# A two-layer graph network: the leftover nodes as row tiles of their own, in all stages

## The chip, the cores and the metric

One core of a Trainium2 chip runs the whole program. The metric is the time of one execution in microseconds (us). "Before" is the kernel as it was, "changed" the kernel under study. All runs quoted have one core, so there is no second die to compare.

## The reference, cut to what matters

```python
# x: 2708 nodes x 1024 features, float32; adj: 2708 x 2708 int32
# layer 0
h = relu(layernorm(x))
f = h @ Wf + bf;  g = h @ Wg + bg
att = softmax(where(adj > 0, relu(f @ g.T), NEG), axis=1)
x = x + att @ (h @ W + bW)
# layer 1
h = relu(layernorm(x));  hw = h @ W1
e = leaky_relu(hw @ a1 + (hw @ a2).T)
x = x + relu(softmax(where(adj > 0, e, NEG), axis=1) @ hw)
```

2708 is 21 x 128 + 20. The 21st full tile and the last 20 nodes are what the change is about.

## The kernel before

Output nodes are taken in five *panels*. For each panel the kernel makes the query side (stage Q), the scores against all nodes (S), the attention-weighted sum of the rows of h (G, "aggregation") and the product with W (P, "projection"). Layer 1 has only G and P. Q, S, G and P are Strassen products of halves: seven products m (M1 to M7) in place of eight. The matmuls of these products are float32, and the trace shows each as two instructions.

Panels were 586, 586, 512, 512, 512 wide. 586 is four tiles of 128 and one of 74:

```python
    wide = (N - 3 * W) // 2                 # 586
    width = [wide, wide, W, W, W]
    ...
    short = [t for t in range(NT) if tiles[t][1] < P]     # the two tiles of 74 rows
    n0, n1 = (tiles[t][1] for t in short)                 # 74, 74
    NM = P - n0                                           # 54
    NY = n1 - NM                                          # 20
    LEFT, MONO, TINY = NQ, NT, NT + 1
```

As *input* rows (of the scores and the aggregation) the 148 leftover nodes were regrouped: MONO is 74 + 54 = 128 rows, TINY the last 20. As *output* rows of the projection they stayed two tiles of 74, a Strassen pair of their own:

```python
        if p == panel_of[short[1]]:
            n = tiles[short[1]][1]
            todo.append((*short, n, [carry[:, e, :, :n] for e in range(2)], col(full, n)))
```

So layer 1's f2 of those nodes (the dot product of a row with a vector) was made in one arrangement and used in the other, and small DMAs carried it over:

```python
    def left_f2():
        a, b = (f[1][:, t:t + 1] for t in short)
        store(f[1][:n0, MONO:MONO + 1], a[:n0])
        store(f[1][n0:, MONO:MONO + 1], b[:NM])
        for g in range(P // B32):
            store(f[1][B32 * g:B32 * g + NY, TINY:TINY + 1], b[NM:n1])
        nc.vector.tensor_scalar(f2s[:, MONO:], f[1][:, MONO:], ALPHA, None, op0=OP.mult)
```

Row work like this is kept in a list (`put`) and handed out in small portions (`behind`) between the matmuls of the next stage. In the scores VectorE keeps the order in which the program names its instructions. A *unit* of the scores is one pair of node tiles: eleven a panel, the last of them MONO and TINY. A *spread* is a transpose on TensorE that lays a column of numbers out as a row on all partitions.

The adjacency matrix becomes additive masks, transposed on TensorE; the part of a panel beyond four full tiles is a *tail*:

```python
            if tail:
                ps = bank("mk_ps", (P, 2, W), BF)
                for k in range(2):
                    nc.tensor.transpose(ps[:, k, :tail], m[1][:tail, 0, k], identb[:tail, :tail])
```

## Time and profile before

| | before |
|---|---|
| median (range) of four runs | 3178.63 us (3177.99 to 3184.48) |
| span of the profiled run | 3178.7 us |
| TensorE idle in it | 3178.7 - 3089.0 = 89.7 us |

"Busy" is the union of an engine's instructions in time. A line number such as L1018 is that of the kernel the profile belongs to, so one place has two numbers: the scores are L1018 before and L1052 after; L45 is a helper through which every VectorE instruction goes, so its tile name tells what it is. In the waits, the line reads: who waited, for whom, total us, times, longest us.

### The profile page before, as it was taken

The page shows a single profiled execution, that of the slowest core. Times are in us where ns is not written, and L with a number is a line of the kernel's source. Part 1 is how long each engine was busy: PE and PEld are TensorE (multiplying, and loading weights), DVE is VectorE, ACT ScalarE, POOL GpSimd, SP SyncE. Part 2 cuts the span into 40 slices and gives each one's busy share as a digit, 9 for nine tenths or more (in the row PEclk, how much of TensorE's full clock was granted, in tenths as well). Part 3 has the DMA queues.
Part 4 walks back from the last instruction along what each step waited for, and adds up shares of the span by engine and source line. Part 5 has one row for each costly group of instructions (what it writes and reads, how often), then busy time and mean ns, then how long its engine had stood idle before and what let it go on. Part 6 is the DMA issues. An engine that isn't in the chain of part 4 may idle for free.

```text
span 3178.7 us, 35524 instructions
## 1 busy us (share of the span) xinstructions
PE 3089.0 (97%) x12982; PEld 2283.8 (72%) x12982; DVE 1782.1 (56%) x3561; ACT 504.2 (16%) x855; POOL 406.7 (13%) x547
## 2 busy tenths in 40 slices
PE   8998999999999989999999999997999999999998
PEld 5576677667876578886888885864767748778684
DVE  7867576375722665517672357657574472644612
ACT  4412120010200101101020002203131130211200
POOL 3724102110002220011000101021010000000000
PEclk9999999999999989999999999998999999999999
DMA  6857839676446566567755567596555455665655
GB/s 248 325 204 281 276 133 340 202 243 211 149 125 185 184 226 204 154 199 238 245 173 154 165 203 228 195 301 221 201 169 178 143 171 170 192 200 171 214 157 196
DMA packets 272487, 649.76 MB, mean 204 GB/s; under 512 B 38016, under 2 KB 104584, under 8 KB 272312
## 3 DMA queue, kind: packets, MB, share of 16 engines
q1 hardware_dynamic: 231320, 523.52, 51.7%
q0 software_dynamic: 40992, 123.96, 11.2%
q8 instruction: 103, 1.69, 0.2%
q14 instruction: 72, 0.59, 0.1%
HBM read 534.53 MB, written 112.83 MB: 204 GB/s over the span
## 4 chain that ended last, share of the span: by engine, by line
PE 86%; issue 6%; DVE 3%; DMA 2%; POOL 1%; ACT 0%; SPq 0%; POOLq 0%; DVEq 0%; ACTq 0%
PE gy L537 11%; PE gz L537 11%; PE gx L537 11%; PE sz L1018 7%; PE pz L916 6%; PE sy L1018 5%; PE gv L537 5%; PE sx L1018 4%; PE px L916 4%; PE py L916 4%; PE M_ps L469 3%; PE qz L537 3%; PE qx L537 2%; PE qy L537 2%; PE mk_ps L693 1%
## 5 line engine op out<-in xcount | busy, mean ns | idle before, releaser
L1018 PE MATMUL sz<-B,As 128*128 128x256 f32 (+1 forms) x1200 | 296.5, 396 | 4.6 <-DVE st L45 3.4
L1018 PEld LDWEIGHTS sz<-B,As 128*128 128x128 f32 x1200 | 229.2, 192 | 53.3 <-DVE st L45 4.8
L1018 PE MATMUL sx<-B,As 128*128 128x256 f32 (+1 forms) x800 | 203.1, 397 | 16.6 <-DVE sm L45 11.5
L849 POOL TENSOR_TENSOR gT<-gT,rr 128x2048 f32<-128x2048 f32 (+3 forms) x20 | 69.8, 3491 | 1144.1 <-DVE rr L45 1056.6
L1018 PE MATMUL sy<-B,As 128*128 128x256 f32 (+1 forms) x800 | 201.7, 395 | 4.8 <-DVE st L45 4.8
L537 PE MATMUL gz<-P,hc 128*128 128x256 f32 (+1 forms) x800 | 186.0, 393 | 2.3 <-ACT gT L838 2.3
L537 PE MATMUL gz<-Sa,hc 128*128 128x256 f32 (+1 forms) x800 | 186.0, 393 | 2.3 <-ACT gT L838 2.3
L537 PE MATMUL gx<-P,hc 128*128 128x256 f32 (+1 forms) x800 | 184.4, 392 | 0.3 <-ACT P L1330 0.3
L537 PE MATMUL gy<-T,hc 128*128 128x256 f32 (+1 forms) x800 | 184.2, 391 | 0.0
L1018 PEld LDWEIGHTS sx<-B,As 128*128 128x128 f32 x800 | 149.3, 191 | 45.7 <-DVE sm L45 11.9
L1018 PEld LDWEIGHTS sy<-B,As 128*128 128x128 f32 x800 | 152.2, 191 | 37.3 <-DVE st L45 5.9
L537 PEld LDWEIGHTS gz<-Sa,hc 128*128 128x128 f32 x800 | 151.2, 190 | 36.0 <-ACT gT L838 4.5
L537 PEld LDWEIGHTS gz<-P,hc 128*128 128x128 f32 x800 | 150.9, 190 | 35.7 <-ACT gT L838 4.5
L537 PEld LDWEIGHTS gx<-P,hc 128*128 128x128 f32 x800 | 152.1, 190 | 32.7 <-issue 2.0
L537 PEld LDWEIGHTS gy<-T,hc 128*128 128x128 f32 x800 | 151.7, 190 | 30.9
L916 PE MATMUL py<-w,ps 128*128 128x512 f32 (+1 forms) x352 | 155.7, 593 | 0.0
L916 PE MATMUL pz<-w,ps 128*128 128x512 f32 (+1 forms) x352 | 155.1, 592 | 0.0
L694 ACT COPY mask<-mk_ps 128x1024 bf16<-128x1024 bf16 x55 | 55.7, 1013 | 615.0 <-PE mk_ps L693 274.3
L916 PE MATMUL px<-w,gT 128*128 128x512 f32 x320 | 144.3, 605 | 6.4 <-issue 5.8
L916 PEld LDWEIGHTS pz<-w,ps 128*128 128x128 f32 (+1 forms) x352 | 65.4, 186 | 85.6 <-issue 82.0
L916 PEld LDWEIGHTS py<-w,ps 128*128 128x128 f32 (+1 forms) x352 | 65.2, 186 | 85.2 <-issue 80.3
L916 PEld LDWEIGHTS px<-w,gT 128*128 128x128 f32 x320 | 60.8, 193 | 83.6 <-issue 80.3
(319 smaller groups left out, 4997.6 us busy)
## 6 DMA issues: line engine op xcount, KB each, us to landing
hc<-hg_d SPq DMA_DIRECT2D x350, 512.0 KB
As<-hs_d SPq DMA_DIRECT2D x150, 512.0 KB
w<-wt_d SPq DMA_DIRECT2D x96, 512.0 KB
w<-in_L_gnn_W_dram SPq DMA_DIRECT2D x72, 512.0 KB
md<-md_d SPq DMA_DIRECT2D x56, 512.0 KB
adj_i<-in_adj_dram SPq DMA_DIRECT2D x50, 512.0 KB
hg_d<-g POOLq DMA_DIRECT2D x40, 512.0 KB, 5.2
hs_d<-hsT POOLq DMA_DIRECT2D x40, 512.0 KB, 6.1
```

The source lines that it names most:

```text
L469: nc.tensor.matmul(ps, wfT[a][c // NH][:, c % NH, :], wgT[b][c], start=(c == 0), stop=(c == NC - 1))
L537: nc.tensor.matmul(ps[d], left(m, k, d), right(m, k), start=(start and k == 0), stop=(k == K - 1 and m not in more), skip_group_check=True)
L693: nc.tensor.transpose(ps[:, k, i * P:(i + 1) * P], m[0][:, i, k], identb)
L694: nc.scalar.copy(mk[:, :, :k4 * P], ps[:, :, :k4 * P])
L849: nc.gpsimd.tensor_tensor(of(e, s), of(e, s), by(s, k), OP.mult)
L916: nc.tensor.matmul(ps, left[i][m][:, k, :], w_[k], start=(start and k == 0), stop=(k == NH - 1), skip_group_check=True)
L1018: nc.tensor.matmul(ps[:n, :h], lefts[q][:, i % 2, c, :n], B[m][c // 2][:, c % 2, :h], start=(start and c == 0), stop=(c == NH - 1), skip_g ...
```

## The change

Its intent: make the leftover nodes the same tiles everywhere. MONO is 64 nodes of panel 1 and 64 of panel 2, TINY 20 nodes of panel 3, as input rows *and* as output rows. Then the third Strassen pair of 74 rows becomes one plain tile of 128 (four products) and one of 20, and f2 needs no copies.

```diff
-    wide = (N - 3 * W) // 2
-    width = [wide, wide, W, W, W]
+    NM = P // 2
+    NY = N - NP * W - P
+    width = [W + NM, W + NM, W + NY, W, W]          # 576, 576, 532, 512, 512
 ...
+        def for_other(m, w_):
+            e, start = int(m in (M2, M3)), m in (M1, M5)
 ...
+            for k in range(NH):
+                if other == MONO:
+                    nc.tensor.matmul(ps, carry[:, e, k], w_[k], ...)
+                    continue
+                for g in range(P // B32):
+                    nc.tensor.matmul(ps[B32 * g:B32 * (g + 1)], G[e][:, k, W:W + B32],
+                                     w_[k][:, g * P:(g + 1) * P], ...)
 ...
-            put(0.0, lambda: (left_h(1, *(done_rows[s] for s in mine)), left_f2()))
+            put(0.0, lambda: left_h(1, *(done_rows[s] for s in mine)))
 ...
+        def rows_of_tiny():
+            xs[TINY] = row_halves("x_res")
+            for e in range(2):
+                nc.gpsimd.memset(xs[TINY][e], 0.0)
+                for ps, _ in places[TINY]:
+                    nc.gpsimd.dma_start(xs[TINY][e][ps], x1_d[TINY][:, e * W:(e + 1) * W])
+            rows_done(TINY, xs[TINY])
```

The inner loop over g is the "four column groups": the 20 rows are weights of 32 columns, and four such sets stand side by side in the array, each with another quarter of 128 columns of W. The result lies as four quarters on the partitions 0, 32, 64, 96, so the 20 rows go through DRAM once to become whole rows again. (The diff is cut; the rest adapts loads, stores and columns.)

## The prediction

> **What bounds the kernel now.** I began with the busy times of the page, because they say whether there is anything but TensorE to look at.
>
> ```profile
> PE 3089.0 (97%) x12982; PEld 2283.8 (72%) x12982; DVE 1782.1 (56%) x3561; ACT 504.2 (16%) x855; POOL 406.7 (13%) x547
> ```
>
> TensorE is busy for 3089.0 of 3178.7 us, so at most 90 us is idle, and the rest falls only if TensorE gets fewer columns to stream. Then I asked what a column costs. The groups by form give the busy time of each shape:
>
> ```profile
> L537 PE MATMUL gz<-P,hc 128*128 128x256 f32 x480 | 105.7, 380 | 1.4 <-ACT gT L838 1.4
> L537 PE MATMUL gz<-P,hc 128*128 128x293 f32 x320 | 80.3, 411 | 0.9 <-ACT gT L838 0.9
> L916 PE MATMUL pz<-w,gT 128*74 128x512 f32 x16 | 7.2, 592 | 0.0
> ```
>
> The 380 and 592 ns of one instruction include the pipeline, so I divide busy time by count: 105.7/480 = 220 ns for 256 columns, 80.3/320 = 251 ns for 293. Both are 0.86 ns a column, with no fixed part: five panels that add up to 2708 columns cost the same however they are cut. The third row says that a tile of 74 rows costs what one of 128 does (450 ns, with the tail of the last included). The chain in order of time gives the pace without tails:
>
> ```profile
> 1038.76 10.30 PE py L916 x24
> ...
> 1236.40 1.86 PE sz L1096 x32
> 1238.27 1.92 PE sx L1088 x8
> 1240.19 3.45 PE sy L1088 x16
> ```
>
> 24 instructions of 512 columns take 10.30 us, so 429 ns each; a product of one tile (8 instructions, two for each f32 matmul of four K blocks) is 3.43 us. The second row is the scores of the 20 nodes, done in four column groups: 32 instructions of 256 columns in 1.86 us, 58 ns each, a quarter of the 216 ns of the last row (3.45/16). The eight after it take 1.92 and not 1.73 us, so leaving the groups costs about 0.2 us.
>
> Last I looked for the 90 idle microseconds, in the waits of TensorE and then of VectorE (columns: total us, times, longest us):
>
> ```profile
> PE sx L1018 <- DVE sm L45: 11.5, 1, 11.5
> PE mk_ps L693 <- DVE nm L45: 8.0, 6, 2.7
> ...
> DVE f2s L45 <- DMA f<-f: 13.8, 1, 13.8
> ```
>
> The longest wait of all is one event, and the timeline of VectorE and GpSimd in the scores of the third panel shows its cause:
>
> ```profile
> 1156.30 0.17 DVE L45 TENSOR_SCALAR f2s<-f 128x2 f32<-128x2 f32 x1 [13.81 <-DMA f<-f]
> ...
> 1158.78 3.78 PE L1018 MATMUL sx<-B,As 128*128 128x256 f32 x8 [11.46 <-DVE sm L45]
> 1163.97 1.04 PE L693 MATMUL mk_ps<-identb,nm 128*128 128x128 bf16 x8 [1.41 <-DVE nm L45]
> ...
> 1131.43 4.07 POOL L140 DMA_DIRECT2D hgl_d<-x_res  x8 [1.58 <-ACT x_res L289]
> 1138.03 4.04 POOL L140 DMA_DIRECT2D hgl_d<-x_res  x8 [2.53 <-DMA hgl_d<-x_res]
> ...
> 1148.84 3.47 POOL L140 DMA_DIRECT2D f<-f  x7 [1.00 <-DMA hgl_d<-x_res]
> ```
>
> The 128+20 nodes left over are cut out of two tiles of 74 rows. To bring their f2 onto the right partitions the kernel copies it with twelve small DMAs, queued behind 24 small ones of the rows. VectorE takes its instructions in order; it reaches the scaling of f2 at 1142.5 and stands until 1156.3, and TensorE runs out of free accumulators: 11.46 + 1.41 = 12.9 us lost.
>
> **What the Trainium skill says.** "TensorEngine Tiling (Array Packing)", Instruction Overhead, gives about 60 cycles of overhead to each matmul, and its Key Properties say that a change of tiling mode drains the engine. The trace agrees with the second (the 0.2 us above); at 256 columns it shows no overhead, but the change goes to 128, where four groups leave 27 ns for an instruction. "TensorE: Matmul & The Clock Gate", Back-to-back issue gap, puts an issue floor of about 25 ns under small matmuls, so 27 is just possible there. "DMA: Bandwidth & Descriptors", Anatomy of one DMA, gives a DMA from GpSimd a fixed cost of about 2 us, mostly the receipt of the write. Here it is more: eight issues from 1131.43, then the next waits until 1138.03 for one of them.
>
> **The change, part by part.**
>
> 1. *Third Strassen group out of the projection.* Before, the two 74-row tiles are a pair with 7 products of 3.43 us: 24.0 us a layer, 48.0 in two. It goes, all of it on TensorE's path.
> 2. *128 nodes as a plain tile.* Four products (two K halves by two output halves) of 3.43 us: 13.7 a layer, +27.5 in two.
> 3. *20 nodes in four column groups.* Four visits a layer, each 16 matmuls of 128 columns, 32 instructions. Half of 1.86 us is 0.93, plus 0.2 for the switch: 1.13 at best. At the 58 ns of the trace it would be 2.06. I choose 1.4 (37 ns each, as small weight loads and issue take their part): 5.6 a layer, +11.2 in two.
> 4. *The same columns elsewhere.* Scores, query side and aggregation go from 293, 293, 256, 256, 256 to 288, 288, 266, 256, 256 a half; the sum is 1354 in both: 0.
> 5. *Small TensorE work.* The leftover rows are transposed as full tiles: in the chain 16 instructions took 1.03 us for 74 columns and 1.75 for 128, so +0.72 for each of two tiles, +1.4. The third panel now has a tail of 20 columns: 22 mask transposes at some 30 ns (two of 74 columns took 0.07 us) and a few spreads: +1.2.
> 6. *The twelve copies of f2 and the wait go.* The rows now lie on the partitions where f2 is used; the only copy left moves 64 values of f1, in program order nothing on VectorE waits for it soon: -12.9.
> 7. *What is added off TensorE.* The 20 nodes' rows are finished as four quarters, stored by sixteen small DMAs and fetched back by eight before they can be normalized. In the built order this hides behind other row work, but VectorE meets the statistics of that tile in the second unit of the fourth panel's scores, some 30 us after the last quarter is stored (1461 and about 1492 on the old clock). Sixteen to thirty DMAs at 0.55 us of issue and some 5 us to land are 15 to 25 us. It should just fit; I allow +2 for it and for the fuller VectorE there (96 of 138 us busy before, about 10 more after).
>
> Sum: -48.0 + 27.5 + 11.2 + 1.4 + 1.2 - 12.9 + 2 = -17.6 us. From 3179.05 that is 3161.4.
>
> **The rivals.**
>
> *The wait moves to the fourth panel.* The same mechanism, GpSimd's small DMAs ahead of an in-order VectorE instruction, is set up again by part 7. For it: only eight DMAs seem to be in flight at a time, and the round trip goes through HBM. Against it: GpSimd is busy 13% and the order leaves 30 us. If the whole chain were late by 10 us, the time would be about 3171.
>
> *Column groups that do not overlap.* If the four groups of 128 columns ran one after another, an instruction would take 107 ns (429/4), part 3 would be 8 x 3.6 = 29 and not 11 us, and the time 3179: no gain in TensorE at all. Against it stands the 58 ns of the same technique in the scores.
>
> *The stall was masking something.* Without the f2 wait, VectorE's backlog in the third panel (its row work of five tiles) could hold TensorE anyway; the tile of 20 leaves that stage, which speaks against it. Then half of the 12.9 would stay: 3168.
>
> *Everything fits*, with groups at 30 ns and no new wait: about 3156.
>
> **Range and chances.** The sure terms are 1 and 2 (-20.5); the term of the wait is nearly sure to vanish where it is, less sure not to come back. The rivals put the time between 3156 and 3179, mostly under 3172. Runs before spread by 6 us. I take 3161 with a range of 3150 to 3173. Two per cent is 63.6 us: with at most 90 us of idle and 20 us of matmuls to win, faster by over 2% is hardly possible (0.01), and no rival loses more than a few us against before (slower 0.01).
>
> **What would show it.** In the changed profile TensorE's busy time should be about 3082 (6.7 less: 48.0 - 27.5 - 11.2 - 1.4 - 1.2); the second panel's projection about 62 us where it was 73; a visit of the column groups 1.1 to 1.7 us in the timeline; the wait of f2 gone from VectorE's waits, and the 11.5 from TensorE's. Wrong would be: a new wait of VectorE for a DMA at the statistics of x_res over 3 us, a visit over 2 us, or TensorE idle by over 85 us.

## The result, and the profile after

| | before | changed |
|---|---|---|
| median of four runs, us | 3178.63 (3177.99 to 3184.48) | 3166.18 (3162.18 to 3169.59) |
| ratio | | 0.9956 (95%: 0.9939 to 0.9974) |
| profiled span, us | 3178.7 | 3160.3 |

A ratio is the mean time of one kernel's fast runs over that of the other's of the same rounds, so it is not quite the ratio of the medians. Ten later runs of the changed kernel, five on each of two chips, gave 0.9952 and 0.9954. The change is worth about half a per cent, by the verdict of 2% the same.

The busy line of the changed kernel's page:

```profile
PE 3085.6 (98%) x13218; PEld 2290.2 (72%) x13218; DVE 1768.6 (56%) x3561; ACT 505.2 (16%) x872; POOL 411.8 (13%) x552
```

TensorE's busy time fell by 3.4 us and its idle time from 89.7 to 74.7. So most of the gain is idle time, and of the 6.7 us of busy time that were forecast about half is missing. (More is missing from the matmuls: the slow stretch that followed the f2 wait before was busy time too; see b_later.) The waits of TensorE in the changed kernel, the longest three:

```profile
PE mk_ps L700 <- DVE nm L45: 9.6, 7, 3.8
PE mx_ps L739 <- DVE mx L45: 7.1, 1, 7.1
PE px L948 <- issue: 5.8, 1, 5.8
```

The 11.5 us of `sx` are gone. Now the stage where they were, the scores of the third panel, as a stretch of the trace: length, then busy time of each engine with its instructions, then the granted clock (the share of TensorE's full clock that the trace shows as granted), DMA share and GB/s. Before:

```profile
1091.20:1244.50 153.30, 139.91 (x709) 119.74 (x709) 95.73 (x202) 14.07 (x17) 29.09 (x50) 0.94 0.72 234
```

and changed:

```profile
1070.30:1215.40 145.10, 144.69 (x734) 120.09 (x733) 96.97 (x209) 15.25 (x28) 14.16 (x22) 1.00 0.74 241
```

Idle time went from 13.4 to 0.4 us although the panel is 4% wider, and the granted clock from 0.94 to 1.00.

In the projection of the third panel, the chain of the changed kernel (start, us, what) shows the column groups:

```profile
1402.99 7.06 PE px L948 x16
1410.05 1.01 PE po L925 x32
1411.06 7.06 PE px L948 x16
```

A visit (one run of these 32 instructions) is 1.01 us, and the 16 instructions after it take 7.06 and not 6.87: 1.20 us in all.

The whole by stages, each from its first TensorE instruction to that of the next, in us; "changed" is a second profile of it (run a_same, below):

| stage | before | changed | difference |
|---|---|---|---|
| S, panel 1 | 187.0 (idle 16.0) | 182.4 (idle 11.3) | -4.6 |
| S, panel 2 | 160.2 (idle 2.7) | 160.4 (idle 3.8) | +0.2 |
| P of panel 2, layer 0 and 1 | 73.14, 72.20 | 63.37, 61.90 | -9.8, -10.3 |
| S, panel 3 | 153.3 (idle 13.4) | 144.4 (idle 0.4) | -8.9 |
| G of panel 3, layer 0 and 1 | 133.02, 134.29 | 138.03, 139.35 | +5.0, +5.1 |
| P of panel 3, layer 0 and 1 | 49.11, 48.17 | 53.94, 53.00 | +4.8, +4.8 |
| S, panel 4 | 138.0 (idle 1.8) | 139.7 (idle 3.3) | +1.7 |

One row does not fit: panel 2 went from 293 to 288 columns a half, 1.7%. Its scores (157.5 us without the idle) should have become 2.7 us shorter and became 0.8 us shorter with the idle out on both sides; against the kernel "before with the wait put later" (155.8 without idle) they even grew. The chain of one unit of these scores shows why. Before, 74-row tail (the first line is the pace, 8 instructions):

```profile
743.44 1.98 PE sy L1018 x8
745.41 0.45 PE mk_ps L693 x8
745.86 0.07 PE mk_ps L698 x2
745.93 2.06 PE sx L1018 x8
```

Changed, 64-row tail:

```profile
719.23 1.94 PE sy L1052 x8
721.17 0.45 PE mk_ps L700 x8
721.61 0.16 PE mk_ps L705 x2
721.77 2.14 PE sx L1052 x8
```

The two transposes are smaller (64 x 64 in place of 74 x 74) and cost more: 0.16 and not 0.07 us, and the eight matmuls after them 0.20 and not 0.08 over their pace. A unit pays 0.36 in place of 0.15. Panel 3, which had no tail, pays for its 20 x 20 transposes too:

```profile
1108.93 0.14 PE mk_ps L705 x2
1109.07 1.99 PE sx L1052 x8
...
1123.11 1.79 PE sx L1052 x8
```

The sum over 22 units of 64 rows and 11 of 20 is 22 x 0.21 + 11 x 0.29 (0.14 + 0.20, less 0.05 that the full mask transposes leave behind without a tail) = 7.8 us. I had put 0.7 us there.

### The profile page after: what moved, and what is told of

Read it like the earlier page. It is cut to its first block, busy times and chain, and to the rows that moved or that the text cites. A ratio compares the mean times of both kernels' runs of the same rounds, so it can differ in the third digit from the quotient of the medians.

```text
span 3160.3 us, 36134 instructions
## 1 busy us (share of the span) xinstructions
PE 3085.6 (98%) x13218; PEld 2290.2 (72%) x13218; DVE 1768.6 (56%) x3561; ACT 505.2 (16%) x872; POOL 411.8 (13%) x552
## 3 DMA queue, kind: packets, MB, share of 16 engines
q0 software_dynamic: 41024, 124.12, 11.3%
## 4 chain that ended last, share of the span: by engine, by line
PE 87%; issue 6%; DVE 3%; POOL 1%; DMA 1%; ACT 0%; SPq 0%; POOLq 0%; DVEq 0%; ACTq 0%
PE gy L545 12%; PE gz L545 11%; PE gx L545 11%; PE sz L1052 7%; PE pz L948 5%; PE sy L1052 5%; PE sx L1052 5%; PE gv L545 5%; PE px L948 3%; PE M_ps L465 3%; PE qz L545 3%; PE py L948 3%; PE qy L545 2%; PE qx L545 2%; PE po L921 1%
## 5 line engine op out<-in xcount | busy, mean ns | idle before, releaser
L1052 PE MATMUL sz<-B,As 128*128 128x288 f32 (+2 forms) x1200 | 296.7, 397 | 3.2 <-DVE st L45 3.2
L856 POOL TENSOR_TENSOR gT<-gT,rr 128x2304 f32<-128x2304 f32 (+5 forms) x20 | 75.4, 3769 | 1088.4 <-DVE rr L45 1003.1
L1052 PE MATMUL sx<-B,As 128*128 128x288 f32 (+2 forms) x800 | 203.1, 397 | 3.2 <-DMA As<-hs_d 3.1
L1052 PE MATMUL sy<-B,As 128*128 128x288 f32 (+2 forms) x800 | 199.1, 392 | 3.1 <-DVE st L45 3.1
L545 PE MATMUL gz<-P,hc 128*128 128x288 f32 (+2 forms) x800 | 186.0, 393 | 2.3 <-ACT gT L845 2.3
L545 PE MATMUL gz<-Sa,hc 128*128 128x288 f32 (+2 forms) x800 | 186.0, 393 | 2.3 <-ACT gT L845 2.3
L545 PE MATMUL gx<-P,hc 128*128 128x288 f32 (+2 forms) x800 | 185.6, 394 | 0.0
L545 PE MATMUL gy<-T,hc 128*128 128x288 f32 (+2 forms) x800 | 184.2, 391 | 0.0
L948 PE MATMUL py<-w,ps 128*128 128x512 f32 x320 | 143.4, 598 | 0.0
L948 PE MATMUL pz<-w,ps 128*128 128x512 f32 x320 | 141.8, 593 | 0.0
```

Source lines behind the costliest of these rows:

```text
L545: nc.tensor.matmul(ps[d], left(m, k, d), right(m, k), start=(start and k == 0), stop=(k == K - 1 and m not in more), skip_group_check=True)
L856: nc.gpsimd.tensor_tensor(of(e, s), of(e, s), by(s, k), OP.mult)
L948: nc.tensor.matmul(ps, left[i][m][:, k, :], w_[k], start=(start and k == 0), stop=(k == NH - 1), skip_group_check=True)
L1052: nc.tensor.matmul(ps[:n, :h], lefts[q][:, i % 2, c, :n], B[m][c // 2][:, c % 2, :h], start=(start and c == 0), stop=(c == NH - 1), skip_g ...
```

## The experiments

Theory: (A) the gain is the f2 wait; it is larger than its idle time, because the clock is lower after it. (B) The projection's matmuls gain as forecast, but small transposes of 64 rows and fewer give much of it back by switching TensorE's tiling mode. Rivals: the wait was masking a backlog; the quarters of TINY cost something by their DMAs; the short instructions themselves and not the switch are dear.

The first four ran on one chip, where before had a median of 3183.0 us.

**a_same**: the changed kernel again, no edit.

> The changed kernel again, as it stands, to see its spread and to have it on the same chip as the runs that change a part of it. Its four runs so far went from 3162 to 3170 us, where before had 3178 to 3184. If the spread is chance, five more give a mean of 3164 to 3168, ratio 0.995 to 0.997.

Measured: 3165.94 us (3163.32 to 3171.15, five runs), 0.9952 (0.9940 to 0.9965). As expected. The spread of 8 us is the kernel's own; the stage that differs most between profiles of the same code is the first panel's scores (idle 11 to 17 us in the profiles). What decides that was not tried.

**b_later**: the kernel before, copies kept, the waiting instruction later.

```diff
-            put(0.0, lambda: (left_h(...), left_f2()))          # f2s scaled at the end of left_f2
+            put(0.0, lambda: (left_h(...), left_f2()))          # copies only
+            put(12.0, lambda: None)
+            put(0.0, left_f2s)
             put(0.0, met)
```

> The kernel before, with the same twelve copies of f2 but the instruction that waits for them put about two and a half units of the scores later. My theory: the 12.9 us that TensorE lost behind the 13.8 us wait of VectorE come back, and nothing else moves: about 3166 us, 0.996, and no wait of f2s for a DMA in the profile. Rival: VectorE's backlog would have held TensorE there anyway, so that about half returns: 3172, 0.998.

Measured: 3165.35 us (3163.50 to 3165.75, five runs), 0.9947 (0.9934 to 0.9959). No wait of f2s for a DMA is left. The scores of the third panel, as a stretch again:

```profile
1088.64:1225.35 136.71, 136.18 (x711) 117.54 (x709) 97.74 (x209) 14.06 (x17) 30.05 (x51) 1.00 0.79 262
```

They took 136.71 us in place of 153.31: 16.6 us, of which 12.9 is idle time. So the rival (half returns) falls, and the forecast 12.9 was too small by 3.7. Moving one instruction in the old kernel buys as much as the whole change. What the matmuls of the change gain, something else in it must lose.

**a_wait**: the changed kernel with a wait put back.

```diff
+            if k == 1 and t == MONO:
+                dot(fm, done_rows[t], halves(wab[k]))
+                for i in range(0, P, 4):
+                    nc.gpsimd.dma_start(f[1][i:i + 4, c:c + 1], fm[i:i + 4])
+            else:
+                dot(f[k][:, c:c + 1], done_rows[t], halves(wab[k]))
```

> The changed kernel with the wait put back: f2 of the tile of 128 nodes goes through 32 small DMAs of 4 rows each to its place, and VectorE scales it at once after. Theory: 32 issues at 0.5 us and 5 us of landing make a wait of 18 to 25 us on VectorE in the third panel's scores, of which TensorE loses all but 1 to 3 us: 15 to 24 us slower than the changed kernel on the same chip, so 3180 to 3190. Rival: what the change gained came from the matmuls and a wait there is absorbed: within 4 us of the changed kernel.

Measured: 3184.52 us (3181.72 to 3188.52, four runs), 1.0009 to before, 18.6 us slower than a_same. VectorE's wait, and TensorE after it:

```profile
DVE f2s L45 <- DMA f<-fm: 17.4, 1, 17.4
```

```profile
1096.92 3.91 PE L1053 MATMUL sy<-B,As 128*128 128x266 f32 x8 [14.62 <-DVE st L45]
```

A wait of 17.4 us on VectorE idles TensorE for 14.6, and the stage became 17.5 us longer (144.40 to 161.91). The eight matmuls after the gap take 3.91 us where this form takes 1.96 (the lengths of one timeline row, tails included): half speed. Theory A holds in both directions.

**a_flat**: TINY as a plain tile, without column groups.

```diff
-                for g in range(P // B32):
-                    nc.tensor.matmul(ps[B32 * g:B32 * (g + 1)], G[e][:, k, W:W + B32], w_[k][:, g * P:(g + 1) * P], ...)
+                nc.tensor.matmul(ps, G[e][:, k, W:W + B32], w_[k], ...)      # ps: 32 rows x 512
```

(The diff is cut; the rest loads, finishes and stores the rows whole.)

> The changed kernel with the 20 nodes projected as a plain tile of 32 rows by 512 columns in place of four column groups; with it they are also loaded, finished and stored by whole rows, so with fewer small DMAs. Theory: a visit of the groups costs 1.20 us in the trace of the changed kernel, four plain matmuls of 512 columns cost 3.43, so 8 x 2.23 = 17.8 us slower than the changed kernel. Rival: the small DMAs of the four quarters cost something too, and their going pays part of it back: 10 us slower or less.

Measured: 3186.09 us (3184.44 to 3187.28, four runs), 1.0013, 20.2 us slower than a_same. A visit in its chain:

```profile
1413.42 3.55 PE po L924 x8
1416.97 7.07 PE px L947 x16
```

3.55 + 0.20 (7.07 over 6.87) = 3.75 against 1.20 is 2.55 us a visit; eight are 20.4. My 17.8 left out that the plain tile of 32 columns pays at its edges as well. The rival falls: fewer DMAs paid nothing back, so the quarters cost no visible time. And the column groups are worth their trouble: without them the change is no gain.

The next four ran together on another chip, before at 3180.59 us.

**a_mask96**: the tails of the masks with 96 rows.

```diff
+        R = 96 if tail else 0
-            last = adj[r0 + k4 * P:r0 + w]
+            last = adj[r0 + k4 * P:r0 + k4 * P + R]
...
-                    nc.tensor.transpose(ps[:, k, :tail], m[1][:tail, 0, k], identb[:tail, :tail])
+                    nc.tensor.transpose(ps[:, k, :R], m[1][:R, 0, k], identb[:R, :R])
```

(The diff is cut; the loads and the negation take R rows too.)

> The changed kernel with the tails of the masks (64, 64 and 20 rows) read, negated and transposed with 96 rows, of which the first 64 or 20 are used. In the traces the two transposes of a 74-row tail and what follows cost TensorE 0.15 us a unit, those of 64 rows 0.36, those of 20 rows 0.29 where there was nothing. My theory: a tile of 64 rows or fewer puts TensorE into another tiling mode and the switch costs about 0.1 us each way; with 96 rows there is none, a unit costs about 0.17: 22 x 0.19 + 11 x 0.12 = 5.5 us faster than the changed kernel (3160.5 if that is at 3166). Rival: the extra is not the switch but the short instructions and their semaphores, or it hides behind VectorE: within 1 us of the changed kernel, or slower by the wider transposes.

Measured: 3160.14 us (3157.56 to 3162.76, five runs), 0.9933 (0.9920 to 0.9945). Against the changed kernel's 0.9952 that is 0.0019 of 3181, 6.0 us. The same unit in its chain:

```profile
722.06 1.94 PE sy L1053 x8
724.00 0.45 PE mk_ps L701 x8
724.44 0.09 PE mk_ps L706 x2
724.53 2.01 PE sx L1053 x8
```

Transposes that are larger by half take 0.09 in place of 0.16 us, and what follows pays 0.07 and not 0.20. The rival (short instructions are dear in themselves) falls: the same number of instructions, each longer, is cheaper. Without their idle time the scores of panels 2 and 3 lost 1.8 us each. Those of panel 1 lost 2.9, but there profiles of one kernel differ by over 1 us; at panel 2's rate the three make 5.4 (an estimate). The 95% intervals of the two ratios overlap, so it is the chain and the stages that carry this reading. By them small mask transposes are dear, as theory B has it.

**a_spread**: the columns that are spread over partitions, with 96 rows.

```diff
-        return [col[:n, i:i + 1] for i, (_, n) in enumerate(pieces[p])]
+        return [(col[:max(n, 96), i:i + 1], n) for i, (_, n) in enumerate(pieces[p])]
```

(The diff is cut; the rest makes room for the rows that are not used.)

> The changed kernel with the columns that are spread over the partitions (14 tails of 64 and 20) transposed with 96 rows or all in place of 64 or 20. Same theory: 10 x 0.2 + 4 x 0.25, some 2 to 3 us faster than the changed kernel; as small as the spread of the runs, so the trace of those instructions decides: the time to the next instruction should fall from 0.23 and 0.16 us to 0.09 to 0.12, and the next two run at their pace. Rival: no change in either.

Measured: 3160.91 us (3158.69 to 3165.64, five runs), 0.9937. From the start times in the trace: the mean time from such a transpose to the next instruction was 0.23 us (64 rows, ten of them) and 0.16 (20 rows, four), with the next two instructions 0.34 and 0.29 us apart; with 96 rows it is 0.13 (forecast 0.09 to 0.12), and the next are 0.25 apart. Without idle time the stages outside the first scores became 4.0 us shorter than in the changed kernel's first profile and 4.8 than in a_same. So small spreads are dear too. The size is less sure: the ratio is only 0.0015 below a_same's, within the noise, and the clock differs by a us or two between profiles.

**a_turn**: the mask of a unit transposed inside that unit.

```diff
             product(q, M6, Z, True)
             add(t[:n, lo], Z[:n, :h], m1[:n, hi])
+            if q:
+                turn(q)
...
             finish(q, sa, 0)
-            if q + 1 <= LEFT:
-                turn(q + 1)
...
         left_over()
+        turn(LEFT)
```

> The changed kernel with the mask of a unit transposed inside its own unit, after the second product, and not at the end of the unit before, where TensorE waits for VectorE's negation (mk_ps <- nm, 9.6 us in seven waits). Theory: VectorE is only late by a few us there, so the waits go and nothing takes their place: 5 to 9 us faster than the changed kernel. Rival: VectorE is the bound in those units, and the wait returns at the next thing TensorE needs from it (sx <- st or sz <- st): within 2 us.

Measured: 3155.38 us (3153.29 to 3156.14, four runs), 0.9917 (0.9904 to 0.9931). The waits of `mk_ps` for `nm` are no longer among TensorE's waits; one of 2.1 us at `sz` took their place. The second panel's scores became 4.6 us shorter with 3.3 us less idle, so again a wait cost more than its length. VectorE is not the bound of those units; it was asked too early. The gain, 11.1 us by the ratios, is over the 5 to 9 expected.

**a_best**: the three together.

> The last three together. If all three theories hold and add up: 12 to 18 us faster than the changed kernel, 3148 to 3155, ratio to before 0.990 to 0.992. If only the tiling mode holds: 3157 to 3159.

Measured: 3147.10 us (3146.62 to 3148.79, four runs), 0.9894 (0.9878 to 0.9909). They add up within the noise: 6.0 + 4.8 + 11.1 = 21.9 by the ratios, 18.4 measured, a little over the 12 to 18 expected.

The last three ran on a third chip, before at 3181.0 us, to ask what the new layout is worth by itself.

**b_best**: b_later and a_turn's edit, in the old layout.

> The kernel before, in its old layout, with the two repairs that need no new layout: the wait for f2 put later, and the mask transposed in its own unit. It asks what the new layout itself is worth. By the sum: before less 16 us (the f2 wait, as measured) less 8 us (its mask waits, 8.0 us) is 3157, ratio 0.992. The changed kernel with its repairs had 3147, so the layout should be worth some 10 us, which is what its own terms make (48.0 - 27.5 - 9.6 = 10.9). Rival: the layout is worth nothing by itself and the repairs are all: 3147 to 3150.

**a_best2** and **a_same2**: a_best and the changed kernel again, beside it.

> The changed kernel with all three repairs again, on the same chip as the run before this: 3145 to 3150, ratio 0.988 to 0.991, and 8 to 12 us below the old layout with its repairs.

> The changed kernel as it stands, on the same chip again: 3164 to 3168, ratio 0.995 to 0.996.

| | median, us | ratio (95%) |
|---|---|---|
| b_best | 3159.76 (3158.23 to 3160.88) | 0.9933 (0.9920 to 0.9945) |
| a_best2 | 3145.31 (3144.17 to 3146.51) | 0.9887 (0.9872 to 0.9902) |
| a_same2 | 3165.66 (3164.53 to 3171.02) | 0.9954 (0.9942 to 0.9967) |

With the waits and the tails repaired the changed kernel is 14.5 us faster than the old layout with its repairs: more than the 8 to 12 I expected, and the rival (nothing) falls. b_best itself came 2.8 us above its forecast of 3157. But not all of the 14.5 is shown to be the layout's. By stages, the four projections of panels 2 and 3 give -10.1, -10.3, +4.8 and +4.8, -10.8 in all, which is the forecast of the matmuls. Most of the difference between the two profiles lies elsewhere, in the first panel's scores (b_best, then a_best2):

```profile
205.13:396.50 191.37, 174.31 (x810) 132.02 (x809) 129.02 (x249) 33.54 (x60) 49.62 (x65) 0.95 0.79 266
203.54:384.90 181.36, 167.91 (x811) 130.40 (x810) 127.76 (x249) 33.35 (x60) 49.21 (x65) 0.97 0.82 281
```

They are 10.0 us apart: 3.6 in idle time and 6.4 in busy time, at a lower granted clock. All other stages together are 4.2 us shorter. b_later, also in the old layout, took 187.0 us in this stage, and the changed kernel's profiles 181 to 186, so b_best lost something there that the layout does not explain, and no run tried what. An estimate of the layout's own worth is 4.2 us and some 3 for the 1.7% fewer columns in that stage, about 7; the rest is open.

## Why the prediction was right or wrong

The time was forecast as 3161.4 and came as 3166, in the range of 3150 to 3173, and within 2% as said. Two terms were mis-sized most, in opposite directions: small TensorE work by some 9 us and the f2 wait by 3.7. That the total came so near is in part luck.

1. *Third group out (-48.0) and plain tile in (+27.5).* Right. The two projections of panel 2 lost 9.8 and 10.3 us; forecast 20.5, measured 20.1, with the spreads for the next scores included.
2. *Column groups (+11.2).* Right in kind, a little high: I chose 1.4 us a visit; it is 1.20, and eight are 9.6 (the stages say 4.8 a layer). The rival of groups that do not overlap falls, a_flat showing what that would be like. My quoted floor of 25 ns is not contradicted: 1.01 us for 32 instructions is 32 ns each, the edge included.
3. *The same columns elsewhere (0).* Right where only matmuls stand: aggregation became 5.0 and 5.1 us longer in panel 3 and 2.5 shorter in panel 2 of layer 0.
4. *Small TensorE work: "a few spreads: +1.2".* This is the step that failed. I took "22 mask transposes at some 30 ns" from the rate of the 74-row tail, as if cost went with columns. I had even quoted the drain at a change of tiling mode, and applied it to the column groups alone. What stands in its place: the tails of 64 rows went from 0.15 to 0.36 us a unit and those of 20 cost 0.29, 7.8 us by the chain; taking the small form away returned, by the ratios, 6.0 us in the masks and 4.8 in the spreads. With 96 rows a unit pays what one of 74 paid (0.16 and 0.15), so what came back was new. The chain's 7.8 and some 2 to 3 for the spreads, from the start times in a_spread, make the term about 10 us where I had 1.2 (an estimate).
5. *The f2 wait (-12.9).* Mechanism right, size too small: b_later shows 16.6 us. I counted the idle time and forgot the clock. After 11.5 us of idle the next eight matmuls took 3.78 us in the timeline where they take 1.89. "TensorE: Matmul & The Clock Gate" of the Trainium skill says in What's actually happening that the gate goes to half speed after an idle window of about 3.4 us; this trace agrees, with 0.50 of the clock granted from 1150.1 to 1167.1 us, 0.94 over the whole stage and 1.00 there without the wait.
6. *Added off TensorE (+2).* The feared wait for TINY's rows did not come: in the fourth panel's scores VectorE waits for no DMA at all. What did come was 1.5 us more of mask waits in that stage.

With these sizes: -48.0 + 27.5 + 9.6 + 1.4 + 10 - 16.6 + 1.5 = -14.6 us, and by the ratios the changed kernel is 14 to 15 us faster. The sum leaves out the idle time of the first panel's scores (16.0 to 11.3 us in the table), which differs between profiles of one kernel, so it is not closed to better than a few us.

Three slips of the prediction change nothing in this. 3179.05 was one of the four runs of before, whose median is 3178.63. The 3156 of "everything fits" leaves out the switch of 0.2 us; with it, it is 3157.5. And where the f2 wait was, the trace shows ten of the twelve copies behind twenty row stores, not 24.

Shown: the wait's worth, by taking it out of the old kernel and putting it into the new one; the small transposes' cost, by removing it alone. That the cause is the switch of tiling mode is read from the skill's "TensorEngine Tiling (Array Packing)", Key Properties, with what the runs show beside it: 74 and 96 rows pay little (0.15 and 0.16 us a unit), 64 and 20 more (0.36 and 0.29). The runs do not see the mode itself; any other cost that sets in between 74 and 64 rows would look the same.

## What to carry to other kernels

Price a long wait of TensorE at its length plus the slow stretch after it, and before redesigning a layout for it, try to move the instruction that waits. When you cut tiles anew, look at what the small helpers become: a transpose of 64 rows can cost more than one of 74 or 96, so pad with rows that are there anyway. A change whose parts are right can still show little because another part pays it away; a table by stages finds that in minutes.

## What the Trainium skill lacked or had wrong

- "TensorEngine Tiling (Array Packing)", Key Properties: it says that a change of mode drains the engine, but gives no time, and says nothing of small transposes. Here a pair of transposes of 64 rows cost 0.36 us with what follows it (20 rows: 0.29), a pair of 96 rows 0.16 (0.09 + 0.07).
- The same page, When to Use Tiling: that a single tile of 32 weight columns, with nothing beside it, pays at its edges too is not said: 3.75 and not 3.43 us for eight instructions of 512 columns.
- "DMA: Bandwidth & Descriptors", Anatomy of one DMA: about 2 us fixed for a DMA from GpSimd. In the kernel before, the small row stores of the third panel's scores landed 4.9 to 5.8 us after their issue (medians by size), and in a_wait 32 copies of 4 rows kept VectorE waiting for 17.4 us. That GpSimd stopped after eight issues (1131.43 to 1138.03) is the program's own doing: in the trace these DMAs use eight semaphores in turn, and each waits for the landing of the one eight before it.
